# Attention scores of two heads in one matmul: 128 stationary columns in place of two times 64

## The chip, the cores and the metric

The kernel runs on one core of one Trainium2 chip. The metric is device time in microseconds (us) of one execution, as a median of several runs. One further execution was recorded by the hardware profiler; every duration below comes from that record.

## The reference, cut to what matters

The kernel computes one block of a Perceiver-like model on `x` of 32 sequences, 64 tokens and 512 features: a cross attention to a context, a latent self-attention (the part that matters here), and a feed-forward layer. In the self-attention each of 16 heads has a query of two parts, one of 128 numbers (`q_nope`, folded into the latent space) and one of 64 numbers that is rotated (`q_pe`). All heads share one key of the same two parts:

```python
q_nope = jnp.einsum('bshd,hdc->bshc', q_nope, wkv_b[:, :NOPE])
scores = (jnp.einsum('bshc,btc->bsht', q_nope, kv) + jnp.einsum('bshr,btr->bsht', q_pe, k_pe)) / math.sqrt(QKD)
scores = jax.nn.softmax(scores + mask, axis=-1)
out = jnp.einsum('bsht,btc->bshc', scores, kv)
```

For one head and one sequence the scores are a 64 x 64 matrix: 64 queries against 64 keys, with a sum over 128 numbers for the first part and, as the kernel lays it out, over 128 more for the rotated one (its cosine and sine products side by side).

## The kernel before, in words

The kernel has stages that follow each other on TensorE. Stage A (to about 241 us) does the cross attention, and projects the tokens to `qa_hi`/`qa_lo` (the latent queries, split into two parts of reduced precision that add up to float32), to `kv` and to `kT`, the keys transposed. Stage B, the self-attention, follows (241 to 562 us), then the output projection, the up and the down projection.

Stage B is a loop over 32 units. A unit is four heads (two pairs, `pj` = 0 and 1) and 256 tokens (four sequences, `b` = 0 to 3). What one unit does on TensorE, in program order:

- `b_q`, L666 to L697, for each pair: `psq`, the first query part of both heads, 18 matmuls of 256 moving columns (L165 to L167 in the helper `mm3`), then `pse`, the rotated part of both heads, 9 more. ScalarE copies `psq` with a bias into one tile `qn` per head (L686), VectorE multiplies `pse` by cosine and sine into one tile `qe` per head (L690, two instructions of 64 partitions each). Between the two pairs stand the four transposes `pst` of an earlier unit's softmax (L738).
- `b_v`, L743 to L755: four matmuls `psv` with an earlier unit's weights, each on 64 rows of the array (L752).
- `b_s`, L699 to L720: the scores `pss`. For each pair, each sequence and each query part there are two matmuls (L708), one per head `j`. A matmul takes the head's 64 queries as its stationary operand and 64 columns of `kT` as its moving operand, and writes 64 partitions of the output: 0 to 63 for the first head, 64 to 127 for the second. That is 2 x 4 x 2 x 2 = 32 matmuls in a unit. VectorE then scales and masks the scores (`s`, L713) and takes their maximum (`mx`, L717); GpSimd subtracts it (L718), ScalarE takes the exponential (L719), and so on in `b_d`.

These matmuls have float32 operands. The profile shows two records of `MATMUL` and two of `LDWEIGHTS` (the load of the stationary operand) for each of them; for a matmul on the split operands (`psq`, `pse`), and for a transpose, it shows one of each.

The order of instructions on an engine is the order of the program with a scheduler's changes. In units 0 and 1 it puts the score matmuls between pieces of the next `psq` and `pse`; from unit 2 on each unit has `psq`, `pse`, `pst`, `psq`, `pse`, `psv`, `pss` in this order. The tiles `qn` and `qe` come from a pool of six buffers each (L554); a unit uses four of each. GpSimd and SP prepare weights and store `v` during this stage (L141, L576 to L589, L767 to L769); the change does not touch them.

Of the kernel before, what the change touches and what calls it, by code (L numbers as in the profile page):

```python
# [9 lines left out]
FP = mybir.dt.float32  # L10
# [8 lines left out]
P = 128  # L19
B, S, D = 32, 64, 512  # L20
# [8 lines left out]
TB = 256  # L29
# [43 lines left out]
def perceiver_block(ctx: ExitStack, tc: tile.TileContext, x, mem, mask, wq_a, bq_a, qnw, wq_b, bq_b,  # L73
                    wkv_a, bkv_a, kvnw, wkv_b, wo, bo, gate, up, down, expert, gamma, beta, cs, out):
    nc = tc.nc

    def pool(name, bufs=1, **kw):
        return tc.tile_pool(name=name, bufs=bufs, reuse_waits="tile", **kw)
# [48 lines left out]
    def after(ins):  # L127
        return tc.issue_after(ins.ins) if ins is not None else ExitStack()
# [28 lines left out]
    def banks(pool, nm):  # L157

        return [pool.tile([P, 2, TB], FP, tag=f"p{i}", name=f"{nm}_{i}") for i in range(4)]

    def mm3(ps, pairs):

        n = len(pairs)
        for j, (ah, al, bh, bl) in enumerate(pairs):
            nc.tensor.matmul(ps, ah, bh, start=(j == 0), stop=False)  # L165
            nc.tensor.matmul(ps, al, bh, start=False, stop=False)  # L166
            nc.tensor.matmul(ps, ah, bl, start=False, stop=(j == n - 1))  # L167


    with ExitStack() as mla:  # L170
        res = mla.enter_context(pool("res"))
        kv = res.tile([P, NT, KVLR], FP, name="kv")
        kT = res.tile([P, 2, B * S], FP, name="kT")
        cq = res.tile([P, 2, 256], FP, name="cq")
        qa_hi = res.tile([P, NKQ, B * S], FR, name="qa_hi")
        qa_lo = res.tile([P, NKQ, B * S], FR, name="qa_lo")
        bqn = res.tile([P, H], FP, name="bqn")
        bqp = res.tile([P, NHP], FP, name="bqp")
# [17 lines left out]
        with ExitStack() as pa:  # L196
# [41 lines left out]
            def prep_wa(j, raw):  # L238
                n = P if j < 4 else 64
                ps = psT.tile([P, NKD, P], FP, tag="T", name=f"psa{j}")  # L240
                for k in range(NKD):
                    nc.tensor.transpose(ps[:, k, :n], raw[:n, k * P : (k + 1) * P], ident[:n, :n])
                sl = slice(j * P, j * P + n)
                return split(wa_hi[:, :, sl], wa_lo[:, :, sl], ps[:, :, :n])
# [238 lines left out]
            for i in range(NT + 2):  # L483
                q, r = i - 2, i - 1
# [10 lines left out]
                if do_q:  # L495
                    qk = ap.tile([P, 576], FP, tag="qk", bufs=1, name=f"qk{q}")
                    xh, xl, _ = xx.pop(q)
# [30 lines left out]
                if i < 2:  # L528
                    for j in range(3 * i, min(3 * i + 3, 5)):
                        last = prep_wa(j, raws[j])  # L530
# [14 lines left out]
        with ExitStack() as pb:  # L545
            pq, pc = ExitStack(), ExitStack()
# [4 lines left out]
            sp = pb.enter_context(pool("b_s", 4))  # L551
            pp = pb.enter_context(pool("b_p", 2))
            vp = pb.enter_context(pool("b_v", 2))
            qp = pq.enter_context(pool("b_q", 6))  # L554
            wqs[1] = pq.enter_context(pool("b_w1", 2))
            ps_v = pb.enter_context(pool("b_psv", 3, space=PSUM, side="right"))
            ps_q = pq.enter_context(pool("b_psq", 3, space=PSUM))
# [108 lines left out]
            def b_q(u, between=None):  # L666
                g, blk = u
                tok = slice(blk * TB, (blk + 1) * TB)
                qs, behind = [], None
                for pj in range(2):  # L670
                    p = 2 * g + pj
                    qh, ql = wqt[p]
                    ps = ps_q.tile([P, 2, TB], FP, tag="q", name=f"psq_{g}_{blk}_{pj}")
                    for j in range(2):
                        c = slice(j * P, (j + 1) * P)
                        mm3(ps[:, j, :], [
                            (qh[:, k, c], ql[:, k, c], qa_hi[:, k, tok], qa_lo[:, k, tok]) for k in range(NKQ)
                        ])
                    pe = ps_q.tile([P, TB], FP, tag="q", name=f"pse_{g}_{blk}_{pj}")
                    c = slice(256, 384)  # L680
                    mm3(pe, [(qh[:, k, c], ql[:, k, c], qa_hi[:, k, tok], qa_lo[:, k, tok]) for k in range(NKQ)])
                    for j in range(2):
                        h = 2 * p + j
                        qn = qp.tile([P, TB], FP, tag="qn", name=f"qn_{h}_{blk}")
                        with after(behind):
                            last = nc.scalar.add(qn, ps[:, j, :], bqn[:, h : h + 1])  # L686
                        qe = qp.tile([P, TB], FP, tag="qe", name=f"qe_{h}_{blk}")
                        r = slice(64 * j, 64 * j + 64)
                        for a in range(2):
                            rope = nc.vector.scalar_tensor_tensor(  # L690
                                qe[64 * a : 64 * a + 64, :], pe[r, :], bqp[r, p : p + 1], cq[r, a, :],
                                ALU.add, ALU.mult,
                            )
                        qs.append((qn, qe))
                    if pj == 0 and between:
                        behind = between(rope)
                return qs, (last, rope)  # L697

            def b_s(u, qs):  # L699
                g, blk = u  # L700
                ps = ps_s.tile([P, 2, 4, S], FP, tag="s", name=f"pss_{g}_{blk}")
                for pj in range(2):
                    for b in range(4):
                        sl = slice(64 * b, 64 * b + 64)
                        kt = slice(blk * TB + 64 * b, blk * TB + 64 * b + 64)
                        for a in range(2):
                            for j in range(2):
                                nc.tensor.matmul(  # L708
                                    ps[64 * j : 64 * j + 64, pj, b, :], qs[2 * pj + j][a][:, sl], kT[:, a, kt],
                                    start=(a == 0), stop=(a == 1),  # L710
                                )
                s = sp.tile([P, 8, S], FP, tag="s", bufs=3, name=f"s_{g}_{blk}")
                nc.vector.scalar_tensor_tensor(  # L713
                    s, ps.rearrange("p a b t -> p (a b) t"), 1.0 / math.sqrt(QKD), cm8, ALU.mult, ALU.add
                )
                mx = sp.tile([P, 8], FP, tag="mx", name=f"mx_{g}_{blk}")
                nc.vector.tensor_reduce(mx, s, AX.X, ALU.max)  # L717
                sub = nc.gpsimd.tensor_tensor(s, s, mx.unsqueeze(2).to_broadcast([P, 8, S]), ALU.subtract)  # L718
                nc.scalar.activation(s, s, AF.Exp)  # L719
                return s, sub  # L720
# [11 lines left out]
            def b_t(u, s):  # L732
                g, blk = u
                pt = ps_v.tile([P, 2, 2, P], FP, tag="v", name=f"pst_{g}_{blk}")
                s4 = s.rearrange("p (a b) t -> p a (b t)", a=2)
                for bp in range(2):
                    for pj in range(2):
                        nc.tensor.transpose(pt[:, bp, pj, :], s4[:, pj, bp * P : (bp + 1) * P], ident)  # L738
                t = pp.tile([P, 2, TB], FP, tag="pT", name=f"pT_{g}_{blk}")
                copies.append(nc.scalar.copy(t, pt.rearrange("p b h s -> p b (h s)")))  # L740
                return t
# [32 lines left out]
            qs, ss, loaded = {}, {}, []  # L774
            for j in range(n):
                g, blk = units[j]
                if blk == 0 and g < 3:
                    load_q(2 * g + 2)
                    load_q(2 * g + 3)
                if g == 3 and blk == 3:  # L780
                    cs_wo = [read_slot(k, "wo") for k in range(2)]
                t = []

                def between(behind):
                    if j >= 1:
                        b_d(units[j - 1], ss[j - 1], behind)
                    if j >= 2:
                        t.append(b_t(units[j - 2], ss.pop(j - 2)))
                        return copies[-1]

                qs[j], pins = b_q(units[j], between)
                v = b_w(*b_v(units[j - 2], *t)) if j >= 2 else None
                if g < 3 and 1 <= blk <= 6:
                    split_q(2 * g + 2 + (blk - 1) // NKQ, (blk - 1) % NKQ, pins)
                if g == 3 and blk in (5, 6):
                    put_slot(blk - 5, "wo", cs_wo.pop(0), pins=pins)
                ss[j], sub = b_s(units[j], qs.pop(j))
                if loaded:
                    with after(sub):
                        prep_sums(*loaded.pop(0))  # L800
                if preps:
                    loaded.append(prep_w(*preps.pop(0)))
                if v and j < n - 1:
                    store_v(*v)
# [27 lines left out]
            with after(seven(pss[0], out_units[1][1], *ops[1], part=(0, 4))):  # L832
                t = b_t(units[n - 1], ss.pop(n - 1))
# [180 lines left out]
    with ExitStack() as pu:  # L1014
# [53 lines left out]
        for b in range(NB // 2):  # L1068
# [3 lines left out]
            for n, k in enumerate(ORDER):  # L1072
# [5 lines left out]
                ps = banks(ps_p, f"up{b}_{k}")  # L1078
# [23 lines left out]
                if b == NB // 2 - 1 and n == 2:  # L1102
                    t = xp.tile([P, 7, TB], FR, tag="x", name="xr_c").bitcast(FP).rearrange("p a n -> p (a n)")
# [21 lines left out]
    with ExitStack() as pd:  # L1125
# [79 lines left out]
        for u, (blk, k) in enumerate(out_units):  # L1205
# [12 lines left out]
            if u in (8, 10) or (u > 15 and k == ORDER[4]):  # L1218
                b = DOWN[(u - 8) // 2] if u < 16 else blk
# [62 lines left out]
```

## Time and profile before

| What | us |
|---|---|
| median of 3 runs (lowest to highest) | 1144.81 (1140.77 to 1144.88) |
| the profiled execution's own time | 1144.21 |
| its span, from first to last instruction | 1142.2 |
| stage B, 241.30 to 562.10 | 320.80, TensorE busy in 319.81 |
| one unit of stage B, from 400.42 to 410.54 | 10.12, TensorE busy in 10.12 |
| the same unit: VectorE, ScalarE, GpSimd busy | 6.13, 3.75, 7.75 |

PE is TensorE's matmul, PEld its weight load, DVE VectorE, ACT ScalarE, POOL GpSimd. A line of the timeline has the start in us, the time to the end of the last instruction of the group in us, engine, line, operation, output<-inputs, the shape on the array (rows*columns of the stationary operand), the moving shape, and the number of records merged. Matmuls overlap in the array, so what counts for the pace is the distance from start to start, not the duration of one.

### The profile page before, as it was taken

How to read it: one execution, taken by the hardware profiler on the slowest of the kernel's cores; microseconds unless marked ns; L12 is line 12 of the kernel's file. 1: busy time of each engine (PE TensorE's matmuls, PEld its weight loads, DVE VectorE, ACT ScalarE, POOL GpSimd, SP SyncE). 2: the span in 40 equal slices, each digit the busy share in tenths (PEclk: the TensorE clock that was granted, in tenths of full speed). 3: DMA queues.
4: the chain of work that ended last, by engine and by line, in shares of the span. 5: the costliest groups of instructions: out<-in, count | busy, mean ns of one | idle time of the engine just before them, and what ended most of it. 6: DMA issues, size and time to landing. Idle time of an engine off the chain costs nothing. (4 is left out here: it accounts for less than half of the span.)

```text
span 1142.2 us, 25971 instructions
## 1 busy us (share of the span) xinstructions
PE 1085.6 (95%) x10172; PEld 997.6 (87%) x10172; DVE 784.2 (69%) x1387; ACT 532.6 (47%) x1014; POOL 524.2 (46%) x704
## 2 busy tenths in 40 slices
PE   6999999999999999999899899998899999999996
PEld 4677777689999999999799799998899999998996
DVE  4666666656666666666779666677794568687876
ACT  3444444433344433334465444455335577654552
POOL 2333333316778787764632010002668774064271
PEclk9999999999999999999999999999999999999998
DMA  8667666344686687672698766674666699998961
GB/s 232 222 224 235 203 213 209 107 155 162 221 271 216 237 280 263 237 239 97 209 373 270 244 228 213 215 236 175 199 187 201 218 289 292 317 297 250 275 206 56
DMA packets 197562, 256.24 MB, mean 224 GB/s; under 512 B 18480, under 2 KB 142016, under 8 KB 197440
## 3 DMA queue, kind: packets, MB, share of 16 engines
q1 hardware_dynamic: 192336, 243.54, 65.6%
q10 hardware_dynamic: 4544, 9.18, 2.2%
q0 software_dynamic: 560, 1.87, 0.6%
q8 instruction: 80, 1.31, 0.5%
q14 instruction: 42, 0.34, 0.1%
HBM read 147.45 MB, written 107.09 MB: 223 GB/s over the span
## 5 line engine op out<-in xcount | busy, mean ns | idle before, releaser
L690 DVE SCALAR_TENSOR_TENSOR qe<-pse,bqp,cq 64x256 f32<-64x256 f32 x256 | 123.7, 483 | 82.2 <-PE pse L167 76.1
L1024 PE MATMUL up<-xr,wh_up 128*128 128x256 f32 x896 | 160.2, 281 | 8.5 <-DVE uo L151 5.2
L1024 PEld LDWEIGHTS up<-xr,wh_up 128*128 128x128 f32 x896 | 137.4, 188 | 10.0 <-issue 3.7
L135 DVE TENSOR_TENSOR hl<-c,hl 128x896 fp32r<-128x896 f32 x85 | 98.2, 1161 | 46.1 <-ACT hl L133 44.6
L660 PE MATMUL dp<-wh_down,hl 128*128 128x256 f32 x441 | 123.6, 280 | 4.4 <-DVE hl L135 4.4
L660 PE MATMUL op<-wh_wo,hl 128*128 128x256 f32 x448 | 126.0, 282 | 1.5 <-DVE hl L135 1.2
L661 PE MATMUL op<-wl_wo,hl 128*128 128x256 f32 x448 | 124.8, 280 | 0.0
L1024 PE MATMUL up<-xr,wl_up 128*128 128x256 f32 x448 | 123.8, 280 | 0.0
L661 PE MATMUL dp<-wl_down,hl 128*128 128x256 f32 x441 | 123.1, 279 | 0.0
L659 PE MATMUL op<-wh_wo,hl 128*128 128x256 f32 x424 | 119.0, 281 | 0.0
L659 PE MATMUL dp<-wh_down,hl 128*128 128x256 f32 x417 | 116.6, 280 | 0.8 <-ACT hl L133 0.8
L133 ACT CAST hl<-c 128x896 fp32r<-128x896 f32 x85 | 79.6, 941 | 74.0 <-PE op L661 35.4
L165 PE MATMUL psq<-qa_hi,qh 128*128 128x256 f32 x384 | 112.9, 294 | 0.0
L166 PE MATMUL psq<-qa_hi,ql 128*128 128x256 f32 x384 | 106.8, 278 | 0.0
L167 PE MATMUL psq<-qa_lo,qh 128*128 128x256 f32 x384 | 106.8, 278 | 0.0
L660 PEld LDWEIGHTS op<-wh_wo,hl 128*128 128x128 f32 x448 | 85.3, 190 | 3.2 <-DVE hl L135 3.2
L660 PEld LDWEIGHTS dp<-wh_down,hl 128*128 128x128 f32 x441 | 83.6, 190 | 5.0 <-DVE hl L135 5.0
L661 PEld LDWEIGHTS op<-wl_wo,hl 128*128 128x128 f32 x448 | 85.2, 190 | 0.9
L661 PEld LDWEIGHTS dp<-wl_down,hl 128*128 128x128 f32 x441 | 83.9, 190 | 1.0
L1024 PEld LDWEIGHTS up<-xr,wl_up 128*128 128x128 f32 x448 | 84.2, 188 | 0.0
L113 POOL TENSOR_TENSOR rs_o<-rst_o,mhalf 128x1 f32<-128x1 f32 x16 | 10.5, 676 | 153.8 <-DVE gs L923 74.5
L659 PEld LDWEIGHTS op<-wh_wo,hl 128*128 128x128 f32 x424 | 80.7, 190 | 0.0
(233 smaller groups left out, 3262.1 us busy)
## 6 DMA issues: line engine op xcount, KB each, us to landing
c<-vd SPq DMA_DIRECT2D x60, 448.0 KB, 4.1
cx<-in_ctx SPq DMA_DIRECT2D x32, 512.0 KB, 4.4
vd<-vw SPq DMA_DIRECT2D x30, 512.0 KB, 4.0
hd<-uo SPq DMA_DIRECT2D x105, 128.0 KB, 3.5
hd<-uw SPq DMA_DIRECT2D x23, 512.0 KB, 3.2
dcw<-hd SPq DMA_DIRECT2D x20, 448.0 KB, 6.1
vd<-v SPq DMA_DIRECT2D x30, 256.0 KB, 4.1
c<-hd SPq DMA_DIRECT2D x17, 448.0 KB, 6.6
```

The lines of the kernel that those rows point to most:

```text
L113: pows.append(nc.gpsimd.tensor_tensor(r, t, mhalf[:, 0:n], ALU.pow))
L133: copy = nc.scalar.copy(hi, src)
L135: return copy, engine.tensor_tensor(lo, src, hi.bitcast(FP), ALU.subtract)
L165: nc.tensor.matmul(ps, ah, bh, start=(j == 0), stop=False)
L166: nc.tensor.matmul(ps, al, bh, start=False, stop=False)
L167: nc.tensor.matmul(ps, ah, bl, start=False, stop=(j == n - 1))
L659: nc.tensor.matmul(ps[s // 2][:, s % 2], h[:, a], wh[:, b], start=(k == 0 and s == 6), stop=False)
L660: nc.tensor.matmul(ps[s // 2][:, s % 2], l[:, a], wh[:, b], start=False, stop=False)
L661: ins = nc.tensor.matmul(ps[s // 2][:, s % 2], h[:, a], wl[:, b], start=False, stop=last)
L690: rope = nc.vector.scalar_tensor_tensor(qe[64 * a : 64 * a + 64, :], pe[r, :], bqp[r, p : p + 1], cq[r, a, :], ALU.add, ALU.mult,)
L1024: nc.tensor.matmul(ps[s // 2][:, s % 2], w[:, i, kk], xr[b, 2 * kk + low][:, j], start=(first and m == 0), stop=(last and m == len(parts) ...
```

## The change

The two heads of a pair share one tile. `qn` and `qe` become tiles of 4 sequences x 2 heads x 64 queries, so that a sequence's queries of both heads are 128 neighbouring columns. The same ScalarE and VectorE instructions write them, now in four pieces of 64 columns with a step of 128. The score matmul takes these 128 columns as its stationary operand and writes all 128 partitions at once: 16 matmuls in a unit in place of 32, with the same 64 moving columns. The pool has three buffers of twice the size in place of six.

```diff
-            qp = pq.enter_context(pool("b_q", 6))
+            qp = pq.enter_context(pool("b_q", 3))
...
+                    qn = qp.tile([P, 4, 2, S], FP, tag="qn", name=f"qn_{p}_{blk}")
+                    qe = qp.tile([P, 4, 2, S], FP, tag="qe", name=f"qe_{p}_{blk}")
+                    by_b = lambda t: t.rearrange("p (b s) -> p b s", s=S)
                     for j in range(2):
                         h = 2 * p + j
-                        qn = qp.tile([P, TB], FP, tag="qn", name=f"qn_{h}_{blk}")
                         with after(behind):
-                            last = nc.scalar.add(qn, ps[:, j, :], bqn[:, h : h + 1])
-                        qe = qp.tile([P, TB], FP, tag="qe", name=f"qe_{h}_{blk}")
+                            last = nc.scalar.add(qn[:, :, j], by_b(ps[:, j, :]), bqn[:, h : h + 1])
                         r = slice(64 * j, 64 * j + 64)
                         for a in range(2):
                             rope = nc.vector.scalar_tensor_tensor(
-                                qe[64 * a : 64 * a + 64, :], pe[r, :], bqp[r, p : p + 1], cq[r, a, :],
+                                qe[64 * a : 64 * a + 64, :, j], by_b(pe[r, :]), bqp[r, p : p + 1], by_b(cq[r, a, :]),
                                 ALU.add, ALU.mult,
                             )
-                        qs.append((qn, qe))
+                    qs.append((qn, qe))
...
                     for b in range(4):
-                        sl = slice(64 * b, 64 * b + 64)
                         kt = slice(blk * TB + 64 * b, blk * TB + 64 * b + 64)
                         for a in range(2):
-                            for j in range(2):
-                                nc.tensor.matmul(
-                                    ps[64 * j : 64 * j + 64, pj, b, :], qs[2 * pj + j][a][:, sl], kT[:, a, kt],
-                                    start=(a == 0), stop=(a == 1),
-                                )
+                            nc.tensor.matmul(
+                                ps[:, pj, b, :], qs[pj][a][:, b].rearrange("p j s -> p (j s)"), kT[:, a, kt],
+                                start=(a == 0), stop=(a == 1),
+                            )
```

## The prediction

> **What bounds the kernel now.** I read the page's first part, then busy time by stretches of time, then TensorE's timeline in one unit, and last the rows elsewhere that look like the new matmul. The page and the stretches:
>
> ```profile
> PE 1085.6 (95%) x10172; PEld 997.6 (87%) x10172; DVE 784.2 (69%) x1387; ACT 532.6 (47%) x1014; POOL 524.2 (46%) x704
> ```
>
> ```profile
> 241.30:562.10 320.80, 319.81 (x4138) 301.05 (x4138) 209.37 (x402) 128.27 (x274) 222.07 (x276) 1.00 0.63 217
> ```
>
> ```profile
> 400.42:410.54 10.12, 10.12 (x134) 9.54 (x131) 6.13 (x12) 3.75 (x8) 7.75 (x11) 1.00 0.94 299
> ```
>
> The columns of the last two are the stretch, its length, busy time of PE, PEld, DVE, ACT and POOL with records, the granted clock, and the DMA share and GB/s. The whole of stage B, and one unit in it, are TensorE from end to end at a granted clock of 1.00; the next engine, POOL, has 2.4 us to spare in a unit. So a microsecond that a unit's TensorE work gains or loses is gained or lost by the stage, 32 times. The unit's score block in TensorE's timeline:
>
> ```profile
> 407.42 1.14 PE L752 MATMUL psv<-pT,kv 64*128 64x256 f32 x8
> 408.49 0.34 PE L708 MATMUL pss<-kT,qn 128*64 128x64 f32 x4
> 408.65 0.29 PE L708 MATMUL pss<-kT,qe 128*64 128x64 f32 x4
> 408.77 0.29 PE L708 MATMUL pss<-kT,qn 128*64 128x64 f32 x4
> ...
> 410.28 0.32 PE L708 MATMUL pss<-kT,qe 128*64 128x64 f32 x4
> 410.54 0.39 PE L165 MATMUL psq<-qa_hi,qh 128*128 128x256 f32 x1
> 410.76 0.28 PE L166 MATMUL psq<-qa_hi,ql 128*128 128x256 f32 x1
> 410.88 0.28 PE L167 MATMUL psq<-qa_lo,qh 128*128 128x256 f32 x1
> ```
>
> A group of four records is the two heads' matmuls, two records each. From 408.65 to 410.28 there are 14 groups: 0.116 us for four, 0.029 for a record. In unit 0, where the timeline is less merged, records start in pairs: 249.14 and 249.14, then 249.20 and 249.20, then 249.25 and 249.26. So the two heads run **at the same time**, each in its own 64 columns of the array, and one head's record takes 0.058 us. That the halves do work side by side is seen again at L402 (stationary 128x64, moving 512): 8 records in 1.94 us less the last's 0.59 is 1.35 us for three steps of a pair, 0.45 a pair; the full-width L301 with 512 moving needs 1.02 - 0.59 = 0.43 us from one record to the next. Two half-width records cost what one full-width record costs.
>
> **What the change costs on TensorE.** It replaces 64 half-width records of a unit, done in pairs, by 32 full-width ones, one after the other. The number of steps stays 32; the question is how long a step is. Its moving half is the same 64 columns, 0.058 us a step. Its weight load has 128 columns in place of 64 + 64 side by side. Rows with a float32 stationary operand of 128x128:
>
> ```profile
> 160.40 0.61 PE L272 MATMUL psq<-rkv,rq 128*128 128x128 f32 x4
> 160.84 0.27 PE L276 MATMUL psq<-ident,rpe 128*128 128x128 f32 x1
> ```
>
> ```profile
> 161.31 0.52 PEld L272 LDWEIGHTS psq<-rkv,rq 128*128 128x128 f32 x4 [0.44 <-DVE x L407]
> 161.75 0.14 PEld L276 LDWEIGHTS psq<-ident,rpe 128*128 128x128 f32 x1
> 161.86 0.53 PEld L286 LDWEIGHTS psb<-bqc,rkv 128*128 128x128 f32 x4
> ```
>
> L272 goes on every (160.84 - 160.40)/4 = 0.11 us with 128 moving columns, and there load and moving side are equally long. L286 decides: its moving operand has one column, so nothing but the load can set its pace, and its four loads take 0.53 us less one load's 0.19, 0.34 for three, **0.113 us** each. So the new step is paced by its weight load at 0.113 us, not by its 0.058 us of moving columns. Bounds: 0.110 (transposes, L347: eight loads in 0.91 less 0.14 us, seven steps) to 0.118 (`psq` in this stage, 410.76 to 410.88, with a split stationary operand of the same size).
>
> [...]
>
> Now the ends of the block. Before, it lasts 410.76 - 408.49 = 2.27 us from its first record to the second `psq`; that contains two changes between half width and full width, seen as 0.22 us from the first `psq` to the second where 0.118 is usual. After, only the entry from `psv` (64 rows) to full width is left; the trace has that passage:
>
> ```profile
> 575.14 1.13 PE L752 MATMUL psv<-pT,kv 64*128 64x256 f32 x8
> 576.20 0.50 PE L657 MATMUL op<-wh_wo,hl 128*128 128x512 f32 x1
> 576.54 0.28 PE L660 MATMUL op<-wh_wo,hl 128*128 128x256 f32 x1
> ```
>
> The first record takes 0.34 us to the next; the same one in full width takes 0.22 (577.12 to 577.34). So entry costs about 0.11 more, the first load in the open. `psv` to the next record is the same 1.06 or 1.07. After: 0.11 + 32 x 0.113 + 0.12 = 3.85 us. **Per unit +1.58 us**, with the bounds 1.48 and 1.74. Units 2 to 31 are of this kind: 30 x 1.58 = 47.4 us. In units 0 and 1 the score matmuls are cut in pieces between `psq` and `pse`, with a change of width at each. By the same measure (gap around each piece less the two `psq` steps) unit 0 now pays 0.68 + 2.28 + 1.39 - 3 x 0.235 = 3.65 us and unit 1 1.82 + 1.39 - 2 x 0.235 = 2.74; after, 3.62 each: 0.0 and +0.9. Together **+48.3 us**.
>
> [...]
>
> **Off TensorE.** ScalarE's `qn` (467 ns) and VectorE's `qe` (482 ns) keep their elements and now write with a step. Nearest rows: VectorE's `qa_lo` writes 3 x 128 with a step and `ql` 384 in one piece, both 557 ns; ScalarE's `v` writes with steps in 590 ns, `pT` in one piece in 587. I take nothing; the lower bound is nothing too, as no element goes away. From above: `qe` of the second pair ends 409.52; its first reader, after, comes at 408.49 + 0.11 + 18 x 0.113 = 410.63, so 1.1 us over four instructions are hidden, 0.28 us each; past that each 0.1 us costs 0.4 us a unit. The joined tiles make the first matmul of a pair wait for both heads; that wait (`qe` held `pss` for 0.2 us in total before) lies under the same 1.1 us. The pool holds as many bytes and the same one and a half units. The softmax behind `pss` starts later by as much as the unit grows, and its engines have that much more time. DMA queues keep their issues. No cover is lost.
>
> The profiled execution took 1144.21 us, 2.0 more than its span: 1144.2 + 48.3 = 1192.5. The median is 0.6 higher, so I say **1193 us**.
>
> **Rivals.**
> - *Not slower: the loads hide.* The array's work is the same 32 steps of 64 moving columns. If the load of the next 128 columns ran under the matmul in 0.058 us, a unit would need 0.11 + 1.87 + 0.12 = 2.10, 0.17 less; 30 of these, 1.8 in unit 0 and 0.9 in unit 1 give 1137 us. If it was the number of records that paced them (0.029 each), 0.94 us less a unit again: 1107. It turns at a step of (2.27 - 0.23)/32 = 0.064 us. For it speaks that PEld is less busy than PE in the unit; against it L286, at 0.113 with almost no matmul.
> - *Load and matmul in turn.* If a full-width load can't run beside so short a matmul, a step is 0.113 + 0.058 = 0.171: 5.70 a unit, 30 x 3.43 + 1.8 + 2.7 = 107 us, 1252. [...]
> - *The step in the writes.* If `qe` took 0.6 us more each, 0.32 over its cover, TensorE would wait 1.3 us in each of 30 units: 1231. Against it the equal rows above.
>
> **How the numbers follow.** Forecast 0.86, loads hidden 0.07, in turn 0.03, the writes 0.04. Inside the forecast: a step of 0.110 gives 30 x 1.48 - 0.1 + 0.8 = 45.1 us, 1190; 0.118 gives 30 x 1.74 + 0.1 + 1.0 = 53.3, 1198; entry without its 0.11 takes off 3. I widen to 1183 and 1204 for stalls of TensorE in this stage that come or go (1 us before) and for what I can't see of a load beside the DMA; the rivals, 0.14 in all, lie outside. Half a per cent (5.7 us) is about what a measurement of this kernel can tell from no change. Faster 0.07, same 0.01, slower 0.92.
>
> **What would show it.** Right: `pss` with 1024 records of each kind, 0.113 us apart, about 3.85 us of block, a unit of 11.7 us, stage B of 369, PE as full as now, the first `psq` after the block without its 0.22; every other stage as before. Wrong: records 0.06 or 0.17 apart, `pss` waiting for `qe`, or a granted clock below 1.00 in stage B.

## The result and the profile after

The changed kernel takes 1189.37 us in the median (1185.82 to 1194.66), the kernel before 1142.79 (1138.02 to 1144.88) beside it: a ratio of 1.0418, with a 95% interval from 1.0363 to 1.0472. It is slower, by 46.6 us between the medians. The profiled executions, 1189.4 and 1144.2, differ by 45.2 us, their spans by 45.1.

First the page's busy times and two stretches: stage B up to its last transposes (before, 241.30 to 561.93 is 320.63 us with TensorE busy in 319.64), and one unit. Columns as before.

```profile
PE 1132.0 (95%) x9148; PEld 1048.3 (88%) x9148; DVE 780.9 (66%) x1387; ACT 531.9 (45%) x1014; POOL 522.8 (44%) x704
```

```profile
241.21:607.71 366.50, 366.50 (x3114) 351.31 (x3113) 209.30 (x402) 128.25 (x274) 222.83 (x278) 1.00 0.55 190
430.62:442.26 11.64, 11.64 (x100) 11.13 (x98) 6.13 (x13) 4.15 (x9) 7.74 (x10) 1.00 0.57 211
```

TensorE has 1024 records fewer and is busy 46 us longer. Stage B grew by 45.9 us, so nearly all of the loss is here; the rest of the span is 0.8 us shorter. The other engines do the same work in a longer time. The share of busy TensorE is 95% in both pages: the number that would be looked at first does not show the loss.

The score block in TensorE's timeline, to be held against the one of before:

```profile
430.62 0.43 PE L707 MATMUL pss<-kT,qn 128*128 128x64 f32 x2
430.90 0.39 PE L707 MATMUL pss<-kT,qe 128*128 128x64 f32 x2
431.12 0.39 PE L707 MATMUL pss<-kT,qn 128*128 128x64 f32 x2
...
434.02 0.39 PE L707 MATMUL pss<-kT,qe 128*128 128x64 f32 x2
434.22 0.37 PE L165 MATMUL psq<-qa_hi,qh 128*128 128x256 f32 x1
434.42 0.28 PE L166 MATMUL psq<-qa_hi,ql 128*128 128x256 f32 x1
434.54 0.28 PE L167 MATMUL psq<-qa_lo,qh 128*128 128x256 f32 x1
```

From 430.90 to 434.02 are 14 matmuls, 28 records: 0.111 us a record, where a pair of half-width records, doing the same work, took 0.058. The load records of the 128 columns last 192 ns in the median here, those of 64 columns lasted 138 before (the view of a line: least, median and greatest ns, first and last start):

```profile
L707 PEld LDWEIGHTS pss<-kT,qn x512: 186/192/193, 247.6 to 607.3; 128*128 128x128 f32 x171
```

```profile
L708 PEld LDWEIGHTS pss<-kT,qn x1024: 132/138/138, 246.8 to 561.6; 128*64 128x64 f32 x171
```

The 54 ns between them, for 64 columns more, are about the difference between the two steps. From the first score record to the second `psq` it is 3.80 us in place of 2.27. Who waits stands in the list of waits (who, for whom; us in total, times, longest):

```profile
DVE s L712 <- PE pss L707: 72.3, 31, 2.9
```

Before it was 15.7 us in 14 waits: VectorE's first step of the softmax now waits for the scores in nearly every unit, as they come 1.5 us later. No `pss` waits for `qe` or `qn` any more.

### The profile page after: what moved, and what is told of

Same layout as the page of the kernel before. It is cut to its first block, busy times and chain, and to the rows that moved or that the text cites. A ratio compares the mean times of both kernels' runs of the same rounds, so it can differ in the third digit from the quotient of the medians.

```text
span 1187.3 us, 23927 instructions
## 1 busy us (share of the span) xinstructions
PE 1132.0 (95%) x9148; PEld 1048.3 (88%) x9148; DVE 780.9 (66%) x1387; ACT 531.9 (45%) x1014; POOL 522.8 (44%) x704
## 5 line engine op out<-in xcount | busy, mean ns | idle before, releaser
L707 PE MATMUL pss<-kT,qn 128*128 128x64 f32 x512 | 100.5, 278 | 0.0
L707 PE MATMUL pss<-kT,qe 128*128 128x64 f32 x512 | 99.0, 275 | 0.0
L718 ACT ACTIVATE s<-s 128x512 f32<-128x512 f32 x32 | 20.2, 632 | 158.1 <-POOL s L717 158.1
L660 PEld LDWEIGHTS op<-wh_wo,hl 128*128 128x128 f32 x448 | 85.6, 191 | 2.4 <-DVE hl L135 2.3
L707 PEld LDWEIGHTS pss<-kT,qn 128*128 128x128 f32 x512 | 77.6, 192 | 9.9 <-issue 9.9
```

The costliest lines, as they stand in the source:

```text
L660: nc.tensor.matmul(ps[s // 2][:, s % 2], l[:, a], wh[:, b], start=False, stop=False)
L707: nc.tensor.matmul(ps[:, pj, b, :], qs[pj][a][:, b].rearrange("p j s -> p (j s)"), kT[:, a, kt], start=(a == 0), stop=(a == 1),)
```

## The experiments

The theory: a full-width float32 weight load takes 0.11 us and sets the pace; two half-width ones go on side by side with their matmuls (0.058 us a pair). The rivals: the stepped writes and joined tiles; the moving side of a full-width matmul; the number of records (a fixed price for each, whatever its size). Blocks below are from the first score record to the next `psq` (2.05 us before, 3.59 in the changed kernel), units are means of 29 distances from one start of `psv` to the next (10.05 and 11.56).

### The layout alone

On the changed kernel:

```diff
-                            nc.tensor.matmul(
-                                ps[:, pj, b, :], qs[pj][a][:, b].rearrange("p j s -> p (j s)"), kT[:, a, kt],
-                                start=(a == 0), stop=(a == 1),
-                            )
+                            for j in range(2):
+                                nc.tensor.matmul(
+                                    ps[64 * j : 64 * j + 64, pj, b, :], qs[pj][a][:, b, j], kT[:, a, kt],
+                                    start=(a == 0), stop=(a == 1),
+                                )
```

> The joined tiles and their stepped writes as in the change, but two score matmuls of 64 stationary columns as before. If the full-width weight load is the whole cause, this is the kernel before in time: 0.029 us a record, 2.05 us from the first score record to the next psq, 10.0 to 10.1 us a unit, 1143 us within 5. If the stepped writes or the joined tiles cost, it is at or near 1189, with units of 11.6 us or waits of pss for qe or qn.

Measured: 1142.84 us against 1144.21 of the kernel before on the same chip, ratio 0.9991 (0.9966 to 1.0016). Block 2.05, unit 10.04:

```profile
426.85 0.34 PE L708 MATMUL pss<-kT,qn 128*64 128x64 f32 x4
...
428.90 0.38 PE L165 MATMUL psq<-qa_hi,qh 128*128 128x256 f32 x1
```

The tiles' writers, from the view of their lines, with least, median and greatest ns:

```profile
L691 DVE SCALAR_TENSOR_TENSOR qe<-pse,bqp,cq x256: 474/483/494, 243.6 to 558.6; 64x256 f32<-64x256 f32 x128
```

```profile
L688 ACT ACTIVATE qn<-psq,bqn x128: 454/466/497, 242.9 to 556.4; 128x256 f32<-128x256 f32 x128
```

Before they took 482 and 467. The layout costs nothing that can be measured; the whole loss is in the shape of the matmul.

### The moving side doubled, full width and half width

On the changed kernel, and in the same manner on the kernel before:

```diff
-                        kt = slice(blk * TB + 64 * b, blk * TB + 64 * b + 64)
+                        w = min(b + 2, 4)
+                        kt = slice(blk * TB + 64 * b, blk * TB + 64 * w)
...
-                                ps[:, pj, b, :], qs[pj][a][:, b].rearrange("p j s -> p (j s)"), kT[:, a, kt],
+                                ps[:, pj, b:w, :], qs[pj][a][:, b].rearrange("p j s -> p (j s)"), kT[:, a, kt],
```

> The change with 128 moving columns in three of four score matmuls: the keys of the next sequence too, and the next matmul writes that part of the scores anew, so the scores that are used are the same. If the weight load of 128 columns sets the step, the moving side may double for nothing: 0.112 us a record still, 3.6 us of block, about 1189 us, and at most 1195. If the moving side sets the step, 24 of 32 records in a unit take twice 0.112: 2.7 us more in a unit, 81 to 86 us more in all, about 1272.

> The same doubling of the moving columns on the kernel before (64 stationary columns a head). If the half-width pairs are at their moving side's rate already (0.058 us a pair of records, load and moving equally long), 24 of 32 pairs take 0.112: 1.3 us more in a unit, 41 us more in all, about 1184 us. If the pairs are paced by their number or by their loads, no change up to the point where the moving side is longer: 1143 to 1150.

Measured: full width 1189.87 us, half width 1184.05, against 1144.21 of the kernel before. The two timelines, full width first:

```profile
431.72 0.39 PE L708 MATMUL pss<-kT,qe 128*128 128x128 f32 x2
431.94 0.39 PE L708 MATMUL pss<-kT,qn 128*128 128x128 f32 x2
432.17 0.39 PE L708 MATMUL pss<-kT,qe 128*128 128x128 f32 x2
432.39 0.39 PE L708 MATMUL pss<-kT,qn 128*128 128x128 f32 x2
```

```profile
437.52 0.39 PE L709 MATMUL pss<-kT,qe 128*64 128x128 f32 x4
437.74 0.39 PE L709 MATMUL pss<-kT,qn 128*64 128x128 f32 x4
437.96 0.39 PE L709 MATMUL pss<-kT,qe 128*64 128x128 f32 x4
```

In full width a record goes on every 0.111 to 0.112 us with 128 moving columns as with 64, and the block is 3.59 us in both: about half of each step was empty on the moving side in the changed kernel. In half width a pair of records went from 0.058 to 0.110 (0.22 for four), the block to 3.24, 40 us in all: before the change the array had no such room. With 128 moving columns both shapes have the same pace.

### The two heads in turn

On the kernel before:

```diff
-                for pj in range(2):
-                    for b in range(4):
...
-                        for a in range(2):
-                            for j in range(2):
+                for j in range(2):
+                    for pj in range(2):
+                        for b in range(4):
...
+                            for a in range(2):
```

> The kernel before with the score matmuls of one head of each pair all ahead of those of the other, so that neighbours in the queue use the same 64 columns of the array. If the two halves' working side by side is what made 0.029 us a record, a record now takes 0.058: 64 of them 3.7 us, block 3.9, 1.85 us more in a unit, about 1202 us. If a half-width record costs 0.029 by itself, nothing changes: 1143. If a load can't run beside a matmul in the same half, 0.11 a record: 6.9 us of block, about 1295.

Measured: 1195.32 us, block 3.70, unit 11.64. Its timeline:

```profile
433.88 0.28 PE L708 MATMUL pss<-kT,qn 128*64 128x64 f32 x2
434.00 0.28 PE L708 MATMUL pss<-kT,qe 128*64 128x64 f32 x2
434.12 0.28 PE L708 MATMUL pss<-kT,qn 128*64 128x64 f32 x2
434.24 0.28 PE L708 MATMUL pss<-kT,qe 128*64 128x64 f32 x2
```

The same matmuls in another order: 0.117 us for two records, where four took 0.116. So the order of heads in the loop is what let the two halves work at once, and a record costs 0.058 in its half, not 0.029 by itself. This is what the theory asks for, and it rules out that the number of records alone sets the pace: it is 64 in both. The expected 1202 was 7 us too much: where the queue passes from one head to the other the two halves overlap (eight records in 0.28 us at 435.29 in place of 0.47), so the block is 0.2 us shorter than I summed, 6 us in 30 units.

### The moving side halved, full width and half width

On both kernels, for `kt` and the output, with `s` built from the 32 computed keys:

```diff
-                        kt = slice(blk * TB + 64 * b, blk * TB + 64 * b + 64)
+                        kt = slice(blk * TB + 64 * b, blk * TB + 64 * b + 32)
...
-                                ps[:, pj, b, :], qs[pj][a][:, b].rearrange("p j s -> p (j s)"), kT[:, a, kt],
+                                ps[:, pj, b, 0:32], qs[pj][a][:, b].rearrange("p j s -> p (j s)"), kT[:, a, kt],
...
-                nc.vector.scalar_tensor_tensor(
-                    s, ps.rearrange("p a b t -> p (a b) t"), 1.0 / math.sqrt(QKD), cm8, ALU.mult, ALU.add
-                )
+                for u in range(2):
+                    t = slice(32 * u, 32 * u + 32)
+                    nc.vector.scalar_tensor_tensor(
+                        s[:, :, t], ps.rearrange("p a b t -> p (a b) t")[:, :, 0:32], 1.0 / math.sqrt(QKD), cm8[:, :, t],
+                        ALU.mult, ALU.add,
+                    )
```

> The change with 32 moving columns in place of 64: the scores of keys 32 to 63 of each sequence aren't computed, those of keys 0 to 31 stand in for them (VectorE reads them twice, in two instructions of half the size). If the weight load of 128 columns sets the step, half the moving side saves nothing: 0.112 us a record, 3.6 us of block, about 1189 us. If the moving side sets it, 0.056 a record: 1.8 us less in a unit, about 1133 us.

> The same halving on the kernel before (64 stationary columns a head, two heads side by side; keys 32 to 63 not computed). If a load of 64 columns takes about half of one of 128, 0.053 to 0.058 us, it now sets the pace of a pair: still 0.029 us a record, 2.05 us of block, about 1143 us. If the pairs were paced by their moving side alone, 0.015 to 0.02 a record: 0.6 to 0.95 us less in a unit, 1113 to 1125 us.

Half width came as expected: 1141.79 us against 1147.30 beside it, ratio 0.996 (0.9918 to 1.0002), block 2.02; half the moving columns save nothing.

```profile
428.06 0.29 PE L708 MATMUL pss<-kT,qn 128*64 128x32 f32 x4
428.17 0.29 PE L708 MATMUL pss<-kT,qe 128*64 128x32 f32 x4
428.29 0.29 PE L708 MATMUL pss<-kT,qn 128*64 128x32 f32 x4
```

This fits a load of 64 columns that takes about 0.058 us, with two of them at the same time, as do the 54 ns between the load records above and the expectation's 0.053, which is the difference between the two steps (0.111 - 0.058). It isn't shown by itself: a least time of 0.029 us for any record would give the same pace here, and no run of half-width records with few moving columns in one half alone tells the two apart.

Full width kept its block at 3.59 us in 23 of 29 units (up to 3.94 in the others), which is the theory's point, but the time was 1224.89: 36 us over the first expectation, 92 over the second. The loss is nearly all after the block. Stretches of that kernel, a block and what follows it:

```profile
434.00:437.40 3.40, 3.40 (x31) 3.40 (x31) 0.92 (x2) 1.07 (x2) 2.17 (x4) 0.98 0.91 272
437.40:440.80 3.40, 3.40 (x18) 3.40 (x18) 1.44 (x3) 0.09 (x1) 1.81 (x3) 0.52 0.83 243
440.80:444.00 3.20, 3.20 (x30) 3.20 (x29) 1.44 (x3) 1.97 (x4) 2.70 (x4) 1.00 1.00 308
```

```profile
438.07 0.41 PE L166 MATMUL psq<-qa_hi,ql 128*128 128x256 f32 x1
438.28 0.41 PE L167 MATMUL psq<-qa_lo,qh 128*128 128x256 f32 x1
438.50 0.41 PE L165 MATMUL psq<-qa_hi,qh 128*128 128x256 f32 x1
```

The granted clock (third column from the end) falls to 0.52 for the 3.4 us after the block, and `psq` goes on every 0.21 us in place of 0.113 to 0.118. The 20 of 29 units that this hits take 13.0 to 13.2 us, the others, with the same block, 11.4 to 11.6; what spares these is open. TensorE shows no idle time in any of the three stretches. Its array was little used all the same: by an estimate, 32 moving columns take half of the 0.058 us of 64, in a step of 0.112 that the load sets, so about a quarter of the block. In the changed kernel, with 64 columns, the granted clock was 1.00 over the 3.4 us behind the block (434.22 to 437.60).

### The block in two halves

On the 32-column kernel, the second pair's scores come after `psv` instead of after the first pair's:

```diff
-                v = b_w(*b_v(units[j - 2], *t)) if j >= 2 else None
+                scores = b_s(units[j], qs.pop(j))
+                next(scores)
+                v = b_w(*b_v(units[j - 2], *t)) if j >= 2 else None
...
-                ss[j], sub = b_s(units[j], qs.pop(j))
+                ss[j], sub = next(scores)
...
                 for pj in range(2):
+                    if pj == 1:
+                        yield
...
-                return s, sub
+                yield s, sub
```

> The 32-column kernel of the run before (keys 32 to 63 not computed), with the score block in two halves of 1.8 us and the four psv matmuls (1.06 us, 256 moving columns) between them. If the fall of the granted clock there (0.91 in stage B, psq at up to 0.182 us a record after the block) came from 3.6 us on end with the array only a quarter used, the clock stays at 0.99 to 1.00, psq at 0.113 to 0.118, and the time is near the change's, 1187 to 1196 us. If the clock falls for another reason, such as the share of used array over a whole unit, the time stays near 1225.

Measured: 1189.16 us, units of 11.35 to 11.56, and in stage B, where the granted clock was 0.91 before the split (241 to 620 us):

```profile
241.00:610.00 369.00, 366.07 (x3127) 351.84 (x3126) 213.27 (x439) 131.97 (x281) 218.23 (x279) 1.00 0.56 195
```

The same loads and the same 32 columns, and the clock stays at 1.00. So the share of little-used array in a unit is not enough to lower it, for that share is the same in both; what differs is that one such stretch lasts 1.8 us in place of 3.6, with `psv` in between. How long a stretch the clock bears was not tried. With the clock out of the way, 32, 64 and 128 moving columns all give 1189 to 1190 us in full width (1.040 to 1.042 times the kernel before beside them).

## Why the prediction was right, point by point

The forecast change of 48.3 us came out at 46.6 between the medians and 45.2 between the profiled executions. Of the 3.6 us between 1193 and 1189.37, 2.0 are that the kernel before had a median of 1142.79 here and not 1144.81.

- **What bounds.** TensorE sets stage B, busy in 366.50 of 366.50 us, and what the score blocks gained is what the stage gained (sum below).
- **The step of the weight load.** Forecast 0.113 us from the bias matmul with one moving column, measured 0.111. That the moving side does not set it is shown by 32, 64 and 128 columns at the same pace; that a load of 64 columns takes no more than 0.058 us, and that the two halves had worked side by side, by the heads in turn (0.117 us for two records). That load and moving side are equally long at 128 columns, as said of L272, is an estimate; the nearest measured are the 0.111 us here and the 0.110 of a half-width pair with 128 moving columns.
- **The ends of the block.** Here I was off. I put the entry's open load at 0.11 us; the first two records take 0.28 where 0.22 is usual, so it is 0.06. And I took the 0.22 us from the first `psq` to the second for a change of width that would go. It is 0.20 still, after a block that is full width like `psq`: that share of it was never the width's. What the width cost at the exit stood one step earlier: from the last group of `pss` to the first `psq` it was 410.54 - 410.28 = 0.26 us where a group takes 0.116, and is 434.22 - 434.02 = 0.20 now where a matmul's two records take 0.22. In sum 1.53 us a unit for a forecast of 1.58, or 1.5 us too much in all.
- **Units 0 and 1.** By the measure of the forecast, 2.25 + 1.79 - 0.47 = 3.57 and 2.23 + 1.79 - 0.47 = 3.55 us, for a forecast of 3.62 each. Against the kernel before that is -0.1 and +0.8, for a forecast of 0.0 and +0.9.
- **Off TensorE: nothing.** Shown by the layout alone, and by `qn` and `qe` at 466 and 482 ns in the changed kernel.
- **Stalls.** TensorE's 1.0 us of idle time in stage B before is 0.0 after. Of it 0.25 us is a wait for `qe` in unit 0, which the gaps of that unit hold already, and 0.7 are two waits of `pse` for `qn`. That they go because the tiles come in time in a longer unit is probable, not shown. I had it in the range, not in the sum.

The sum 30 x 1.53 - 0.1 + 0.8 - 0.7 = 45.9 stands against 45.9 measured in stage B. All three rivals are refuted: the hidden load (0.058 us a step) and load and matmul in turn (0.171) by the 0.111 us measured, the stepped writes by the layout alone.

Nothing here points to a kernel faster than both: in half width, halving the 64 moving columns saved nothing and doubling them cost 40 us, so the load and the moving side look equally long there. A shorter load was not tried.

## What to carry to other kernels

Fewer matmuls are not less work: before joining two half-width matmuls, compare the load of the stationary columns with the stream of the moving ones, for here a step paced by a load of 128 columns took 0.111 us, and one with two of 64 side by side 0.058. Find the price of a load from a row that has almost no moving columns. Keep neighbours in the queue on different halves of the array: the block took 2.05 us so, and 3.70 with the heads in turn. And where loads set the pace on end, look at the granted clock behind that stretch, not only in it: with 32 moving columns it was 0.98 over 3.4 us of the block and 0.52 over the 3.4 us behind it.

## What the runs showed of the hardware

- The granted clock fell to about half (0.52 over 3.4 us) after 3.6 us of matmuls with 32 moving columns under loads of 128, in 20 of 29 units, with TensorE busy throughout; with 64 columns, or with 1.06 us of `psv` in between, it stayed at 1.00. Moving sides between 32 and 64 columns were not tried.
- `psq` and `pse`, with the same shapes throughout, run at two paces, 0.113 and 0.118 us a record, for whole runs of 27 records, at a granted clock of 1.00 in both: in the kernel before, units of 9.90 us stand in rows beside rows of 10.11, in the changed one 11.43 alternates with 11.63. Which of the two a run gets moves with the kernel. That is 0.2 us a unit, some 4% of these records, and its cause is open.
